# Keys and values brought to token-major form through DRAM squares and VectorE, in a gated delta-rule attention block with a mixture of experts

## The chip, the cores and the metric

The kernel runs on one core of one Trainium2 chip. The metric is the device time of the whole program in microseconds, as the median of several executions. One further execution is recorded by the hardware profiler, and all profile lines come from that one.

## The reference

The program is one layer: layer norm of `x` (2 batches, 2048 tokens, 512 features), plus a gated delta-rule attention, plus a mixture of experts on the first 512 tokens of batch 0.

```python
xn  = layernorm(x)
q = silu(causal_conv4(xn @ Wq) + qcb)      # 16 heads of 128; k and v likewise
k = k * 128 ** -0.5
alpha = sigmoid(xn @ Wa + ba); beta = sigmoid(xn @ Wb + bb)
def step(S, t):                            # per batch and head, over 2048 tokens
    err = S @ k[t] - v[t]
    S = alpha[t] * S - beta[t] * outer(err, k[t])
    o[t] = S @ q[t]
attn = (layernorm_head(o) * ln_w + ln_b) * sigmoid(xn @ Wg) @ Wo
moe  = sum over 4 chosen of 16 experts: down(silu(gate(xn)) * up(xn)) * weight
out  = x + attn + moe
```

Everything is float32.

## The kernel before

The recurrence is done in chunks of 128 tokens (`C`). Inside a chunk the delta rule is a triangular system; its inverse is built from 32 by 32 squares, and only the 128 by 128 state `S` goes from one chunk to the next. A pair is two heads (`HG`), so a batch has 8 pairs; a block is 512 tokens (`BLK`), so a pair has 4 blocks of 4 chunks, and the two batches together have 256 chunks. `recurrence(b, first)` walks over the chunks of a batch, pair by pair, and in every iteration does a little of many things. The order of TensorE, VectorE, ScalarE and GpSimd is written out by hand: each stage is a generator, and `step(...)` in eight slots per iteration advances it. DMAs issued from SP are placed by a scheduler. The stages are:

- `before(n, c)`: what needs no state. In its five first steps it multiplies `q` and `k` (L720), finishes the inverse of the diagonal part (L715, L731, L740, L741, L753), and turns keys and values from feature-major to token-major: four TensorE transposes into one PSUM bank (L735, L736), one ScalarE copy to SBUF (L744), and a GpSimd multiplication that makes `kg` (L750).
- `after(n, c)`, one iteration later: `r` from state and keys (L782, L786), the solve (L793, L797), the new state (L802, L809) and the output `po` (L816, L819), then its mean and variance (L826 to L830). `po` lives in a pool of a single PSUM bank.
- `output(n, c)`, one iteration later still: it normalises `po` (L843), transposes it (L848), gates it (L851, L854) and writes it to DRAM (`oT_d`, L856). It begins with three empty steps, so L843 comes in slot 4.
- `item(n+1, what, h)`: the projection of the next block for q, v or the gate (L156), in halves of two weight tiles; then a causal convolution (`conv_taps`, L131 to L142, and `conv_sum`, three VectorE instructions at L147), then a silu. For q, `gin` (one buffer) is loaded from DRAM by `conv_taps`' caller (L362) and GpSimd multiplies by it (`qg`, L370).
- `key_item(u+2, blk, h)`: the same for keys, two pairs ahead. The keys go to DRAM (`k_d`, L397) and their scores (L206, L210) go to DRAM too (`aT_d`); `inverses` works on those with GpSimd (L246, L249), three steps per iteration in the first ten or so of a pair's sixteen chunks.
- `experts`: the expert matrices (L1154, L1169), four steps per iteration until they are done; `route`: who goes to which expert, in the prologue; `out_chunk`: the last projection by `Wo` (L987), for batch 0 between the two recurrences and for batch 1 woven into the last pair.

`PLAN[c]` names the two items (A, B) of chunk c of a block. A is worked on in slots 2, 4, 5, 6 and 8; B begins in slot 6, becomes `hold`, and is convolved in the next iteration, where `hold` comes in slots 1, 2 and 4. What is left of a generator is drained at the end of the iteration.

`conv_taps` writes the last three tokens of the block before into the front of `raw` with GpSimd (`raw<-halo`, L133), and L147 reads it.

Of the kernel before, what the change touches and what calls it, by code (L numbers as in the profile page):

```python
# [44 lines left out]
def block_kernel(ctx, tc, x, wq, wk, wv, wg, wo, wa, wb, ba, bb, par, consts,  # L45
# [9 lines left out]
    def bank(pool, tag):  # L55
        return pool.tile([P, 512], F32, tag=tag, name=tag)
# [27 lines left out]
    for i in range(1, NQ, 2):  # L84
# [32 lines left out]
           for u in range(NB * NP)]  # L117
    aT_d = [dp.tile([P, NHC, C], F32, name=f"aT_d{u}") for u in range(NB * NP)]
# [169 lines left out]
    PLAN = (("q", 0), ("k", 0)), (("q", 1), ("v", 0)), (("g", 0), ("k", 1)), (("v", 1), ("g", 1))  # L288

    def loads(n):  # L290

        u, blk = blocks[n]
        b = u // NP
        if u not in ws:
            ws[u] = [load_w(bp, tag, w, u % NP * HG, f"{tag}{u}") for tag, w in WS]
        decs = bp.tile([P, HG, CB, DW], F32, tag="decB", name="decB")
        nc.sync.dma_start(
            out=decs, in_=dec_d[b][u % NP][blk].rearrange("p (h c j) -> p h c j", h=HG, c=CB))
        kt = bp.tile([P, HG, BLK], F32, tag="k", name="k")
        nc.sync.dma_start(out=kt, in_=k_d[u][blk].rearrange("h p t -> p h t"))  # L300
        qt = bp.tile([P, HG, BLK], F32, tag="q", name="q")
        qg = bp.tile([P, HG, BLK], F32, tag="qg", name="qg")
        have[n] = (decs, kt, qt, qg, [None] * HG, [])
# [34 lines left out]
    def item(n, what, h, later=None):  # L338


        u, blk = blocks[n]
        b = u // NP
        h0 = (u % NP) * HG
        _, _, qt, qg, vs, _ = have[n]
        ps = bank(ps_p, "p")
        i = "qvg".index(what)
        xt, w = get_xT(b, blk), ws[u][i]
        proj_part(ps, w, h, xt, range(2))
        yield
        proj_part(ps, w, h, xt, range(2, NKT))  # L350
        if (blk, h) == (NBK - 1, HG - 1) and (u + 1) // NP == b:
            tag, w = WS[i]
            ws.setdefault(u + 1, [None] * 3)[i] = load_w(bp, tag, w, (u + 1) % NP * HG, f"{tag}{u + 1}")
        yield
        if what == "g":
            nc.scalar.activation(gate_tile(n)[:, h, :], ps, AF.Tanh, scale=0.5)
            return
        p = 0 if what == "q" else 2
        raw, cv = conv_taps(ps, p, h0, h, blk, later)
        if p == 0:  # L360
            gin = bp.tile([P, BLK], F32, tag="gin", name="gin", bufs=1)
            nc.sync.dma_start(  # L362
                out=gin, in_=gin_d[b][h0 + h, blk * BLK:(blk + 1) * BLK].partition_broadcast(P))
        yield
        conv_sum(raw, cv, p, h0 + h)
        yield
        if p == 0:
            nc.scalar.activation(qt[:, h, :], cv, AF.Silu)  # L368
            yield
            nc.gpsimd.tensor_tensor(qg[:, h, :], qt[:, h, :], gin, ALU.mult)  # L370
        else:
            vs[h] = bp.tile([P, BLK], F32, tag="v", name="v", bufs=4)
            nc.scalar.activation(vs[h], cv, AF.Silu)
# [28 lines left out]
    def projection(n):  # L402

        loads(n)
        for what, h in (("q", 0), ("v", 0), ("q", 1), ("v", 1), ("g", 0), ("g", 1)):
            for _ in item(n, what, h):
                pass
            yield
        load_ops(n)
# [17 lines left out]
    with ExitStack() as es:  # L427
# [34 lines left out]
        def scaled(b, c):  # L462
            mean, r = xns[b, c]
            xn = xns[b, c] = np_.tile([P, HID], F32, tag="xn", name="xn", bufs=3)
            nc.vector.tensor_scalar(xn, xins.pop((b, c)), mean, r, ALU.subtract, ALU.mult)
            if b == 0 and c < FC:
                nc.sync.dma_start(out=xn_d[c * C:(c + 1) * C, :], in_=xn)
# [124 lines left out]
        with tc.manual_schedule(engines={E.PE, E.DVE, E.Activation, E.Pool}):  # L592
            moments(0, 0)
            for g in range(NBK):
                if g + 1 < NBK:
                    moments(0, g + 1)
                if g + 2 < NBK:
                    fetch(0, g + 2)
                for c in range(g * CB, (g + 1) * CB):
                    scaled(0, c)  # L600
                    turned(0, c)
                    if c > 0:
                        gated(0, c - 1)
                if g > 1:
                    key_step(g - 2)
                if 0 < g < 3:
                    key_step(g - 1), key_step(g - 1)
# [16 lines left out]
            r = route(nc, bank, ps_l, mp, cst, cstf[:, N_CONST * P:], topk_idx, topk_w, tw, pos, wrow, trow)  # L624
            inv, firsts = iter(()), []
            for t in range(3, len(keyed) + 3):
                first = t < 11
                old = t - 3
                if t == 11:
                    loads(0)  # L630
                    firsts = [item(0, what, h, later)
                              for what, h in (("q", 0), ("v", 0), ("q", 1), ("v", 1), ("g", 0), ("g", 1))]
# [28 lines left out]
                if first:  # L661
                    n1 += 2
                    if n1 % CB == 0 and n1 // CB + 1 < NBK:
                        fetch(1, n1 // CB + 1)
                        moments(1, n1 // CB + 1)
                    if n1 < NC:
                        scaled(1, n1), scaled(1, n1 + 1)
                if t >= 10:
                    next(r, None)
# [28 lines left out]
    def before(n, c):  # L698
# [4 lines left out]
        decs, kt, qt, _, vs, _ = have[n]  # L703
# [25 lines left out]

        pz = bank(ps_l, "l")  # L730
        nc.tensor.matmul(pz[:, 0:Q], lhsT=op["ihi"][:, c, :], rhs=xs, start=True, stop=True)  # L731

        pkv = bank(ps_l, "l")
        for h in range(HG):
            nc.tensor.transpose(pkv[:, h * D:(h + 1) * D], kt[:, h, cs], ident)  # L735
            nc.tensor.transpose(pkv[:, HW + h * D:HW + (h + 1) * D], vs[h][:, cs], ident)  # L736
# [6 lines left out]
        kv = k2.tile([P, 2, HG, D], F32, tag="kv", name="kv")  # L743
        nc.scalar.copy(kv.rearrange("p s h j -> p (s h j)"), pkv)  # L744
# [4 lines left out]
        kg = k2.tile([P, HG, D], F32, tag="kg", name="kg", bufs=3)  # L749
        nc.gpsimd.tensor_tensor(kg, kv[:, 0], bcast(gd1[b][:, ci, hs], D), ALU.mult)  # L750
# [14 lines left out]
        found[n, c] = (pT, kv, kg, inv)  # L765

    def after(n, c):
# [4 lines left out]
        _, kt, _, qg, _, _ = have[n]  # L772
        pT, kv, kg, inv = found.pop((n, c))
# [3 lines left out]
        if S is None:  # L777
            r = kv[:, 1]
        else:
            pq = bank(ps_c, "c")  # L780
            for h in range(HG):
                nc.tensor.matmul(pq[:, h * D:(h + 1) * D], lhsT=kt[:, h, cs], rhs=S[:, h, :],  # L782
                                 start=True, stop=True)
            r = k2.tile([P, HG, D], F32, tag="r", name="r")
            for h in range(HG):
                nc.vector.scalar_tensor_tensor(  # L786
                    r[:, h, :], pq[:, h * D:(h + 1) * D], gd0[b][:, ci, h0 + h:h0 + h + 1],
                    kv[:, 1, h, :], ALU.mult, ALU.add)
# [44 lines left out]
    def output(n, c):  # L833
# [5 lines left out]
        for _ in range(3):  # L839
            yield  # L840
# [17 lines left out]
    def recurrence(b, first):  # L858
# [13 lines left out]
        mine = {}  # L872
        with tc.manual_schedule(engines={E.PE, E.DVE, E.Activation, E.Pool}):
            for m, at in enumerate([*steps, None, None]):
# [3 lines left out]
                if at:  # L878
# [3 lines left out]
                    if c == 0:  # L882
# [3 lines left out]
                        if blk == 0:  # L886
# [3 lines left out]
                            step(inv)  # L890
                    a = before(n, c)
# [7 lines left out]
                    if u == NB * NP - 1:  # L899

                        if ci == 1:
                            wos = load_wo(b)
                        if ci >= 4:
                            if c == 0:
                                slots.append(big())
                            for _ in last:
                                pass
                            last = out_chunk(b, ci - 4, wos, slots[ci % len(slots)])
                            step(last)
                A, B = pair  # L910
                ps = None

                step(z), step(a), step(hold), step(last)

                step(A), step(z), step(a), step(hold)
# [5 lines left out]
                step(A), step(z), step(a), step(y), step(y), step(y), step(y), step(hold), step(ex)  # L921
# [32 lines left out]
        if slots:  # L954
            for ci in range(NC - 4, NC):
                for _ in out_chunk(b, ci, wos, slots[ci % len(slots)]):
                    pass
# [15 lines left out]
    def out_chunk(b, c, wos, oT):  # L973

        nc.sync.dma_start(out=oT, in_=oT_d[b][c])
        xin = ap.tile([P, HID], F32, tag="aTf", name="xf", bufs=2)
        nc.sync.dma_start(out=xin, in_=x[b, c * C:(c + 1) * C, :])
        if b == 0 and c < FC:
            for j in range(c * TOPK, (c + 1) * TOPK):
                yk = bp.tile([P, HID], F32, tag="v", name="yk", bufs=4)  # L980
# [3 lines left out]
        yield  # L984
        py = bank(ps_p, "p")
        for h in range(H):
            nc.tensor.matmul(py, lhsT=oT[:, h, :], rhs=wos[h], start=(h == 0), stop=(h == H - 1))  # L987
# [8 lines left out]
    slots = [big() for _ in range(NBK - 1)]  # L996
    wos, first = load_wo(0), projection(NP * NBK)
    for c in range(NC):
        for _ in out_chunk(0, c, wos, slots[c % 3 if c < 12 else 1 + c % 2]):
            pass  # L1000
# [6 lines left out]
def route(nc, bank, ps, mp, cst, number, topk_idx, topk_w, tw, pos, wrow, trow):  # L1007
# [29 lines left out]
    run = small("run", NE * n)  # L1037
# [3 lines left out]
    pr = bank(ps, "l")  # L1041
    nc.tensor.matmul(pr[:, 0:NE * n], lhsT=cst[:, K_LT, :], rhs=sel, start=True, stop=False)
    nc.tensor.matmul(pr[:, 0:NE * n], lhsT=cst[:, K_ONE, :], rhs=run, start=False, stop=True)
    pc = bank(ps, "l")
# [19 lines left out]
    at = goes  # L1064
# [37 lines left out]
    pt = bank(ps, "l")  # L1102
# [133 lines left out]
```

## Time and profile before

| | |
|---|---|
| median of 3 executions | 3862.36 us (3862.25 to 3865.29) |
| the profiled execution | 3863.44 us, of it a span of 3861.7 us |
| VectorE, ScalarE, GpSimd busy | 61%, 44%, 44% of the span |
| DMA packets | 583353, of them 354752 under 512 B; 541.36 MB |
| prologue (layer norm, routing, first keys) | 0 to about 245 us |
| recurrence of batch 0, experts until 1377 us | about 245 to 1955 us |
| `Wo` of batch 0 | about 1955 to 2200 us |
| recurrence of batch 1 | about 2200 to 3500 us |
| last pair with `Wo` of batch 1 woven in | about 3500 to 3862 us |

The page gives busy times per engine, the span in 40 slices, the chain of work that ended last, and groups of instructions by line. A float32 matmul is two records in it, and the duration of a record overlaps with that of the next one: the time that a matmul takes from TensorE is the distance between two starts in the timeline, not the duration. In the timeline, `x4` merges four records, and the bracket at the end of a line names the idle time before it and what ended it.

### The profile page before, as it was taken

How to read it: one execution, taken by the hardware profiler on the slowest of the kernel's cores; microseconds unless marked ns; L12 is line 12 of the kernel's file. 1: busy time of each engine (PE TensorE's matmuls, PEld its weight loads, DVE VectorE, ACT ScalarE, POOL GpSimd, SP SyncE). 2: the span in 40 equal slices, each digit the busy share in tenths (PEclk: the TensorE clock that was granted, in tenths of full speed). 3: DMA queues.
4: the chain of work that ended last, by engine and by line, in shares of the span. 5: the costliest groups of instructions: out<-in, count | busy, mean ns of one | idle time of the engine just before them, and what ended most of it. 6: DMA issues, size and time to landing. Idle time of an engine off the chain costs nothing.

```text
span 3861.7 us, 58910 instructions
## 1 busy us (share of the span) xinstructions
PE 3743.5 (97%) x17988; PEld 2439.1 (63%) x17988; DVE 2361.5 (61%) x6136; ACT 1700.4 (44%) x4027; POOL 1690.6 (44%) x3046
## 2 busy tenths in 40 slices
PE   6889999999999999999999999999999999998899
PEld 5557767677676666666654466666666666665454
DVE  5766566665665667777740277777777777663221
ACT  3434444444444455555510155555555555542110
POOL 1246465464654636364520063636363545541010
PEclk9889999999999999999999999999999999999999
DMA  5655656556566554545563335344545444342322
GB/s 162 184 149 162 189 152 190 167 154 191 157 184 170 149 170 108 147 139 163 171 214 113 120 106 139 105 136 112 138 116 127 122 121 133 97 112 76 98 78 88
DMA packets 583353, 541.36 MB, mean 140 GB/s; under 512 B 354752, under 2 KB 425920, under 8 KB 578432
## 3 DMA queue, kind: packets, MB, share of 16 engines
q1 hardware_dynamic: 560928, 456.18, 41.7%
q0 software_dynamic: 22112, 81.41, 7.2%
q8 instruction: 147, 2.41, 0.3%
q14 instruction: 166, 1.36, 0.1%
HBM read 363.69 MB, written 173.67 MB: 139 GB/s over the span
## 4 chain that ended last, share of the span: by engine, by line
PE 84%; DVE 5%; DMA 2%; issue 1%; POOL 1%; ACT 1%; SPq 1%; POOLq 0%; ACTq 0%; DVEq 0%
PE p L156 39%; PE p L987 11%; PE p L1154 4%; DVE cv L147 3%; PE o L816 3%; PE l L720 3%; PE o L819 3%; PE c L793 3%; PE c L802 3%; PE p L206 3%; PE c L782 2%; PE p L1169 2%; PE l L735 1%; PE l L753 1%; PE l L762 1%
## 5 line engine op out<-in xcount | busy, mean ns | idle before, releaser
L147 DVE SCALAR_TENSOR_TENSOR cv<-raw,prm,cv 128x512 f32<-128x512 f32 x1152 | 909.7, 790 | 86.4 <-ACT cv L142 29.5
L156 PE MATMUL p<-xT,wg 128*128 128x512 f32 x1024 | 482.6, 594 | 3.6 <-DVE aTf L210 3.6
L987 PE MATMUL p<-wo,oTf 128*128 128x512 f32 x1024 | 457.9, 602 | 26.4 <-DMA oTf<-oT_d 24.7
L156 PE MATMUL p<-xT,wq 128*128 128x512 f32 x1024 | 482.6, 594 | 0.0
L830 POOL TENSOR_TENSOR rs<-rs,mhalf 128x2 f32<-128x2 f32 x256 | 269.3, 1052 | 483.9 <-DVE rs L829 468.9
L748 POOL COPY inv<-iT 32x32 f32<-32x32 f32 x512 | 103.9, 203 | 861.5 <-DVE iT L740 649.7
L156 PE MATMUL p<-xT,wv 128*128 128x512 f32 x1024 | 481.0, 593 | 0.0
L134 ACT COPY raw<-p 128x512 f32<-128x512 f32 x384 | 223.7, 583 | 525.1 <-PE p L156 510.6
L156 PE MATMUL p<-xT,wk 128*128 128x512 f32 x896 | 431.9, 608 | 16.1 <-DVE aTf L210 11.5
L797 ACT COPY w<-c 128x256 f32<-128x256 f32 x256 | 95.4, 373 | 633.9 <-PE c L793 633.9
L809 DVE SCALAR_TENSOR_TENSOR S<-S,gtot,c 128x128 f32<-128x128 f32 x480 | 145.0, 343 | 357.9 <-PE c L802 357.7
L987 PEld LDWEIGHTS p<-wo,oTf 128*128 128x128 f32 x1024 | 193.1, 193 | 251.1 <-issue 222.7
L249 POOL TENSOR_TENSOR Y<-Y,t 128x30 f32<-128x30 f32 (+14 forms) x480 | 311.0, 648 | 37.6
L142 ACT ACTIVATE cv<-p,prm 128x512 f32<-128x512 f32 x384 | 300.7, 783 | 1.7
L246 POOL TENSOR_TENSOR t<-Y 128x30 f32<-128x30 f32 (+14 forms) x480 | 287.8, 600 | 20.3 <-DMA Y<-aT_d 10.9
L156 PEld LDWEIGHTS p<-xT,wg 128*128 128x128 f32 x1024 | 176.8, 191 | 136.5 <-issue 132.2
L156 PEld LDWEIGHTS p<-xT,wq 128*128 128x128 f32 x1024 | 177.1, 191 | 134.6 <-issue 134.1
L156 PEld LDWEIGHTS p<-xT,wv 128*128 128x128 f32 x1024 | 176.3, 191 | 132.0 <-issue 132.0
L156 PEld LDWEIGHTS p<-xT,wk 128*128 128x128 f32 x896 | 159.6, 196 | 143.5 <-issue 126.3
L786 DVE SCALAR_TENSOR_TENSOR r<-c,gd,kv 128x128 f32<-128x128 f32 x480 | 145.1, 343 | 169.0 <-PE c L782 167.8
L370 POOL TENSOR_TENSOR qg<-q,gin 128x512 f32<-128x512 f32 x128 | 194.3, 1518 | 99.4 <-ACT q L368 99.3
L802 PEld LDWEIGHTS c<-w,kg 128*128 128x128 f32 x1024 | 154.1, 191 | 121.4 <-issue 100.9
(182 smaller groups left out, 7120.8 us busy)
## 6 DMA issues: line engine op xcount, KB each, us to landing
row<-a_d SPq DMA_DIRECT2D x128, 258.0 KB
dec_d<-decA SPq DMA_DIRECT2D x128, 258.0 KB
decB<-dec_d SPq DMA_DIRECT2D x64, 516.0 KB
k_d<-kf SPq DMA_DIRECT2D x128, 256.0 KB
gin<-gin_d SPq DMA_DIRECT2D x128, 256.0 KB
k<-k_d SPq DMA_DIRECT2D x64, 512.0 KB
aT_d<-aTf SPq DMA_DIRECT2D x128, 256.0 KB
oT_d<-oT SPq DMA_DIRECT2D x256, 128.0 KB
```

The costliest lines, as they stand in the source:

```text
L134: nc.scalar.copy(raw[:, KS - 1:], ps)
L142: nc.scalar.activation(cv, ps, AF.Identity, bias=cbias(p, h0 + h), scale=tap(p, h0 + h, KS - 1))
L147: nc.vector.scalar_tensor_tensor(cv, raw[:, j:j + BLK], tap(p, h, j), cv, ALU.mult, ALU.add)
L156: nc.tensor.matmul(ps, lhsT=w[:, k, h * D:(h + 1) * D], rhs=xt[k], start=(k == 0), stop=(k == NKT - 1))
L246: nc.gpsimd.tensor_tensor(t, bass.AP(col.tensor, col.offset, [col.ap[0], (Q, j), (0, n)]), bass.AP(row.tensor, row.offset, [row.ap[0], (0, ...
L249: nc.gpsimd.tensor_tensor(Y[:, 0:j, j + 1:], Y[:, 0:j, j + 1:], t, ALU.add)
L370: nc.gpsimd.tensor_tensor(qg[:, h, :], qt[:, h, :], gin, ALU.mult)
L786: nc.vector.scalar_tensor_tensor(r[:, h, :], pq[:, h * D:(h + 1) * D], gd0[b][:, ci, h0 + h:h0 + h + 1], kv[:, 1, h, :], ALU.mult, ALU.add)
L802: nc.tensor.matmul(pss[:, h * D:(h + 1) * D], lhsT=kg[:, h, :], rhs=w[:, h, :], start=True, stop=True)
L830: nc.gpsimd.tensor_tensor(rs, rs, mhalf[:, 0:HG], ALU.pow)
L987: nc.tensor.matmul(py, lhsT=oT[:, h, :], rhs=wos[h], start=(h == 0), stop=(h == H - 1))
L1154: nc.tensor.matmul(ps[:fn, s, :], lhsT=w[f][:, s, k, :], rhs=xt[:, k, :], start=(k == 0), stop=(k == NKT - 1))
```

## The change

Token-major keys and values are no longer made by TensorE. Each value block is written to DRAM by its item (`v_d`, four blocks in turn), keys are there already, and `squares(n, c)` reads both back for chunk c with eight DMAs of 32 partitions by 8 pieces by 32 numbers (128 bytes a piece). A piece is a row of a 32 by 32 square; the squares land where they belong in the transposed matrix, each still unturned, and one VectorE transpose (which turns 32 by 32 squares in place) for values and one for keys finishes. The four TensorE transposes, the PSUM bank and the ScalarE copy go. `squares` is called two iterations ahead and has three buffers.

For that, values have to come first: `PLAN` and the two other lists of items put v ahead of q, and q0 and q1 now stand as B of chunk 1 and A of chunk 2. `output` loses its three empty steps, and `step(y)` moves to slot 2. In the prologue, the moments and `route` are spread over earlier steps, `route` takes PSUM banks of the tag `p` and the scaling of batch 1 goes from VectorE to GpSimd. The woven `Wo` of batch 1 loads its operand an iteration ahead (`get_out`), in two slots.

```diff
+    v_d = [dp.tile([HG, P, BLK], F32, name=f"v_d{i}") for i in range(4)]
...
-    PLAN = (("q", 0), ("k", 0)), (("q", 1), ("v", 0)), (("g", 0), ("k", 1)), (("v", 1), ("g", 1))
+    PLAN = (("v", 0), ("k", 0)), (("v", 1), ("q", 0)), (("q", 1), ("k", 1)), (("g", 0), ("g", 1))
+    VB = 2
...
+    def squares(n, c):
+
+        u, blk = blocks[n]
+        sq[n, c] = bp.tile([P, 2, HG, D], F32, tag="sq", name="sq", bufs=3)
+        for i, d in enumerate((v_d[n % 4], k_d[u][blk])):
+            for g in range(NQ):
+                o = c * C + g * Q
+                nc.sync.dma_start(
+                    out=sq[n, c][g * Q:(g + 1) * Q, i].rearrange("r h (i j) -> r (h i) j", j=Q),
+                    in_=d[:, :, o:o + Q].rearrange("h (i r) j -> r (h i) j", r=Q))
...
-            vs[h] = bp.tile([P, BLK], F32, tag="v", name="v", bufs=4)
-            nc.scalar.activation(vs[h], cv, AF.Silu)
+            v = bp.tile([P, BLK], F32, tag="v", name="v", bufs=VB)
+            nc.scalar.activation(v, cv, AF.Silu)
+            nc.sync.dma_start(out=v_d[n % 4][h], in_=v)
...
-            nc.vector.tensor_scalar(xn, xins.pop((b, c)), mean, r, ALU.subtract, ALU.mult)
+            (nc.gpsimd if b > 0 else nc.vector).tensor_scalar(
+                xn, xins.pop((b, c)), mean, r, ALU.subtract, ALU.mult)
...
-            r = route(nc, bank, ps_l, mp, cst, cstf[:, N_CONST * P:], topk_idx, topk_w, tw, pos, wrow, trow)
+            r = route(nc, bank, ps_p, mp, cst, cstf[:, N_CONST * P:], topk_idx, topk_w, tw, pos, wrow, trow)
...
-                if t >= 10:
-                    next(r, None)
+                for _ in range({4: 1, 5: 1, 6: 2, 7: 1, 8: 1, 9: 1, 10: 2}.get(t, 0)):
+                    next(r)
...
+        v = k2.tile([P, HG, D], F32, tag="vT", name="vT")
+        kg = k2.tile([P, HG, D], F32, tag="kg", name="kg", bufs=3)
+        for i, t in enumerate((v, kg)):
+            nc.vector.transpose(t.rearrange("p h j -> p (h j)"), sq[n, c][:, i].rearrange("p h j -> p (h j)"))
+
         pz = bank(ps_l, "l")
         nc.tensor.matmul(pz[:, 0:Q], lhsT=op["ihi"][:, c, :], rhs=xs, start=True, stop=True)
-
-        pkv = bank(ps_l, "l")
-        for h in range(HG):
-            nc.tensor.transpose(pkv[:, h * D:(h + 1) * D], kt[:, h, cs], ident)
-            nc.tensor.transpose(pkv[:, HW + h * D:HW + (h + 1) * D], vs[h][:, cs], ident)
         yield
...
-        kv = k2.tile([P, 2, HG, D], F32, tag="kv", name="kv")
-        nc.scalar.copy(kv.rearrange("p s h j -> p (s h j)"), pkv)
...
-        kg = k2.tile([P, HG, D], F32, tag="kg", name="kg", bufs=3)
-        nc.gpsimd.tensor_tensor(kg, kv[:, 0], bcast(gd1[b][:, ci, hs], D), ALU.mult)
+        nc.gpsimd.tensor_tensor(kg, kg, bcast(gd1[b][:, ci, hs], D), ALU.mult)
...
-        for _ in range(3):
-            yield
         o = k2.tile([P, HG, D], F32, tag="o", name="o")
...
+        squares(*steps[0]), squares(*steps[1])
...
+                    if m + 2 < len(steps):
+                        squares(*steps[m + 2])
                     a = before(n, c)
...
+                    if ci > 3:
+                        last = out_chunk(b, ci - 4, wos, *got)
+                    if ci >= 3:
+                        got = get_out(b, ci - 3, slots[(ci - 3) % 2])
...
-                step(A), step(z), step(a), step(hold)
+                step(A), step(z), step(a), step(y), step(hold)
...
-                step(A), step(z), step(a), step(y), step(y), step(y), step(y), step(hold), step(ex)
+                step(A), step(z), step(a), step(hold), step(ex)
...
+    def get_out(b, c, parts):
+
+        heads = []
+        for t, n in parts:
+            o = len(heads)
+            nc.sync.dma_start(out=t, in_=oT_d[b][c][:, o:o + n, :])
+            heads += [t[:, h, :] for h in range(n)]
         xin = ap.tile([P, HID], F32, tag="aTf", name="xf", bufs=2)
         nc.sync.dma_start(out=xin, in_=x[b, c * C:(c + 1) * C, :])
+        return heads, xin
```

## The prediction, made before the changed kernel ran

> **What bounds the kernel.** I read the page's busy times first, then the timeline by engine for two blocks, then the waits, then the chain of waits at the end.
>
> ```profile
> PE 3743.5 (97%) x17988; PEld 2439.1 (63%) x17988; DVE 2361.5 (61%) x6136; ACT 1700.4 (44%) x4027; POOL 1690.6 (44%) x3046
> ...
> PEclk9889999999999999999999999999999999999999
> ```
>
> TensorE is busy all the time at full granted clock, so what leaves its queue counts in full as long as nothing else arrives late. How much leaves must not be read from durations (272 to 289 ns each); starts tell it:
>
> ```profile
> 2459.72 0.31 PE L731 MATMUL l<-xs,ihi 128*128 128x32 f32 x2
> 2459.86 0.31 PE L735 MATMUL l<-unit,k 128*128 128x128 f32 x1
> 2460.00 0.27 PE L736 MATMUL l<-unit,v 128*128 128x128 f32 x1
> 2460.11 0.27 PE L735 MATMUL l<-unit,k 128*128 128x128 f32 x1
> 2460.23 0.27 PE L736 MATMUL l<-unit,v 128*128 128x128 f32 x1
> 2460.33 1.88 PE L156 MATMUL p<-xT,wg 128*128 128x512 f32 x4
> ```
>
> The four transposes take 2460.33 - 2459.86 = 0.47 us. Starts of L782 lie 11.05 and 11.94 us apart in turn without experts (with scores the longer), 14.6 us with them.
>
> **What goes.** Transposes: 256 chunks x 0.47 = **-120**. Two more waits of TensorE go:
>
> ```profile
> PE p L987 <- DMA oTf<-oT_d: 24.7, 6, 8.2
> ...
> PE o L816 <- DVE o L843: 13.8, 21, 1.8
> ```
>
> L843 two slots earlier frees the only `po` bank earlier: **-14**. `Wo`'s operand an iteration ahead: -24.7, and the slow matmuls after these gaps, of which this is the first:
>
> ```profile
> 3509.51 6.54 DMA oTf<-oT_d
> 3516.10 6.58 PE p L987 x8
> ...
> 3525.46 3.44 PE p L987 x8
> ```
>
> 6.58 against 3.44, then 5.67, 5.40, 5.40 and 3.70: -9.6 more, together **-34**. Prologue: VectorE is over 90% busy from 150 to 230 us; routing (about 30 us of it) moves to 90 to 150 us, where VectorE idles some 24 us, and 8 us of scaling go to GpSimd. GpSimd's `inverses` (160 to 223 us) then bound the stretch, so I take **-10** (bounds +5 and -25). Sum -178.
>
> **What comes, and what hides it.** *VectorE*: two 128x256 transposes a chunk. Nearest rows: the 128x32 transpose, 211 ns; copies from PSUM of 32, 128 and 256 columns at 179, 292 and 424 ns, so 1.1 ns a column: 211 + 224 x 1.1 = 0.46; from SBUF less. Bounds 0.3 and 0.9 (two passes); I take 0.42, 0.85 a chunk. They stand just ahead of L740, which waits 208 us in all, 0.81 a chunk, for L731. Counted from L782 in the new order: `r`, `xs` and `pT` end at 1.7, the two L843 at 2.4, `hold`'s convolution (2.45) at 4.85, transposes at 5.7, `top` at 5.95; L753 needs it at 6.48. Covered, with half a microsecond to spare. Without that cover a chunk would pay what the transposes run over. The new `PLAN` puts two convolutions in both chunk 1 and chunk 2 (before: 1 and 3), so chunk 2 needs 11.1 us of VectorE (5.1 and two times 2.42 for convolutions and 1.15 for `decA`) in TensorE's 10.6; chunk 3 starts half a microsecond late on VectorE. That lies inside the wait found below and is not counted twice. ScalarE's 150 us of copies (L744) and the PSUM bank go at no gain: neither is waited for. `kg` comes from SBUF and no later.
>
> *DMA engines*: per chunk 8 x 256 pieces of 128 bytes. Nearest row: the loads of `Y` (same pieces) at 252 to 256 us, where queue 1 had
>
> ```profile
> q1 hardware_dynamic: 3360, 0.42, 69.6%
> ```
>
> 0.696 x 4 us x 16 engines / 3360 = 13.3 ns a packet; 2048 x 13.3 / 16 = 1.7 us a chunk, and 0.4 for writing v. The windows show a share of 0.45 in batch 1 (5.2 us a chunk) and 0.59 beside experts: 7.3 of 11, not a bound. The Trainium skill ("VectorE: DVE Perf Modes", The three transpose paths) speaks against it: a plain DMA that transposes by its access pattern is 19 times slower than the crossbar. By that rule, 256 KB at its 435 GB/s (my estimate, from "DMA: Bandwidth & Descriptors", Specifications) x 19 = 11 us a chunk, on top of 5.2: 16 us, over 1100 us slower. I take the row: 32 numbers stay contiguous on both sides here.
>
> *SP*: its issues in batch 1 sum to 22.5 us per block of 46.2; 34 more at 0.5 (`Y`'s: 0.48, plus 0.04) make 39.5 of 44: tight. SP also stands until a `v_d` write has landed before it loads those squares, some 2.5 us a time, with `oT_d`, `inv` and `row` behind it; but nothing in its queue is wanted sooner than an iteration later, except `gin`. At the first handover (240 to 262 us), where SP issues without a pause, 16 of the 24 first squares stand ahead of `X_d` and cost nothing; the rest is within the prologue's bounds.
>
> *GpSimd and gin*: here I expect the new wait. `gin` has one buffer. Before, q0 and q1 ended in different iterations; now both are drained at the end of chunk 2, and the built order has `qg x2` adjacent on GpSimd, q1's `gin` load waiting on GpSimd on SP, and behind both `qg` the `raw<-halo` copy that chunk 3's convolution (k1) on VectorE waits for, with both transposes, L740, L741 and so L753 behind it. One `qg` already costs VectorE a wait, in this chunk with experts (started 787.31):
>
> ```profile
> 788.09 1.28 POOL L370 TENSOR_TENSOR qg<-q,gin 128x512 f32<-128x512 f32 x1
> 789.30 0.19 POOL L133 COPY raw<-halo 128x3 f32<-128x3 f32 x1
> ```
>
> and on VectorE
>
> ```profile
> 789.53 2.81 DVE L147 SCALAR_TENSOR_TENSOR cv<-raw,prm,cv 128x512 f32<-128x512 f32 x3 [0.47 <-POOL raw L133]
> ```
>
> A `gin` load: issued 2318.89, its traffic is the last block of
>
> ```profile
> DMA  0079931999994000044445564335520000210721
> ```
>
> (2318 to 2323 us, 0.125 a slice), ending at 2321.75: 2.9, with receipts 3.1. Without experts, the first `qg` ends 1.95 after chunk 3's L782 where inverses stand ahead of it (from the one at 2456.40), load at 5.15, second `qg` 6.4, `raw` 6.6, convolution 9.1, transposes 9.95, `top` 10.2; L753's turn is at 6.48: TensorE stands 3.75. In a pair's last block, without inverses (1.85 less), 1.9. Mean 0.75 x 3.75 + 0.25 x 1.9 = 3.3. Beside experts: the row above plus 4.4 gives `raw` 793.7, `top` 797.5 against L753's 796.84 - 0.47: 1.15 in three of four, about 1 with GpSimd's expert requests. Blocks with keys to make: 56, of which 20 beside experts (until 1377 us). **+118 and +20.** Bounds: 0 (if the load is quick or VectorE late anyway) and 5 us a block (280).
>
> Clock: the skill ("TensorE: Matmul & The Clock Gate", Why this matters for your kernels) wants no gaps over about 3 us. Rows: gaps of 5.4 to 6.5 cost 0.3 to 3.1, one of 1.14 cost 0.2 (10.57 for 24 matmuls, 10.3 otherwise). By the rule 27 gaps of 3.75 would pay some 1.9 each, 51; I take 0.2, **+5**, since 3.75 is nearer the cheap side of these rows.
>
> **Sum.** -178 + 138 + 5 = -35. The profiled execution had 3863.4 (span 3861.7), 1 us over the median: 3863 - 35 = **3828**.
>
> **Rivals.**
> - *The wait is absorbed* (bound 0): 3863 - 178 = 3685. For it: VectorE has 13% left. Against: the order on three engines is fixed, and the round trip has no other cover. 0.16.
> - *SP becomes the bound*, the slower side. Place: blocks of batch 1 and the 12 of batch 0 after the experts. At 0.76 an issue (four `ihi` loads behind a megabyte of `X_d` writes took 3.05) a block takes 22.5 + 34 x 0.76 = 48.3 instead of 46.2: 40 x 2.1 = +84, with tail, prologue and expert blocks -60: 3885; at 1 us an issue 56.5 a block, 4200. It decides above (46.2 - 22.5) / 34 = 0.70 an issue. For it: each DMA reuses one of eight semaphores and waits for the eighth before it. Against: `Y`'s eight in a row went at 0.54. 0.20.
> - *Transposes at 0.9*: +0.95 a chunk; chunks 1 and 2 lose 0.5 each (+40), chunk 3 one (+50): 3918. 0.12.
> - That the transposes stay on TensorE is excluded by the built order, which has 1024 fewer.
>
> **Numbers.** Forecast 0.52 (3790 to 3865 is its own range). The range 3700 to 3940 leaves out most of the first rival and SP's far end. Within 0.2% (8 us) is what this measurement can't tell from no change. Faster: 0.44 of the forecast's, 0.16, 0.02 = 0.62; same 0.04 + 0.02 + 0.02 = 0.08; slower 0.04 + 0.16 + 0.10 = 0.30.
>
> **What will show it.** L735 and L736 gone and L731 followed by L156 0.14 later; a TensorE wait at L753 (or its weights) for VectorE's `top` in one chunk of four, about 3 us, and GpSimd idle before the second `qg` by a DMA of `gin`, about 60 times 3; no `oTf` wait; L816's wait gone; the 128x256 transposes near 0.4; SP's issues of `sq` near 0.5. Wrong would be: GpSimd not idle before `qg`, or TensorE waiting for `ilo`, `inv`, `row` or `sq`, which would be SP or the DMA engines.

## The result, and the profile after

The changed kernel takes **4188.5 us** (median of 4 runs, 4183.5 to 4199.3) against 3862.3 us before on the same chip: ratio **1.085**, 95% interval 1.083 to 1.088. It is slower by 326 us; 3828 was forecast, with a range that ended at 3940.

First the page of the kernel after (engine, busy time, share, instructions; then the granted TensorE clock in 40 slices):

```profile
PE 3749.3 (90%) x16964; PEld 2393.1 (57%) x16964; DVE 2559.2 (61%) x6632; ACT 1541.0 (37%) x3771; POOL 1672.6 (40%) x3062
...
PEclk9989999999999999999999999999999999999999
```

The instructions fell as announced (17988 to 16964 on TensorE), yet TensorE is as long busy as before (3749 us against 3744; the slow clock below ate the saving) and idle for another 432 - 118 = 314 us: the span grew from 3861.7 to 4181.7. The mean granted clock fell from 0.989 to 0.953. A view of the waits (engine, tile, line, releaser: us in total, times, longest) says where it stands:

```profile
PE l L769 <- DVE top L760: 306.5, 56, 13.9
PE c L502 <- POOL xn L481: 22.8, 5, 11.0
```

L769 is the old L753. It stands for `top` 56 times: in the last chunk of 55 of the 56 blocks with keys to make, and once more, for 1.68 us, in another chunk. The chain behind it is in the same view of GpSimd and of VectorE:

```profile
POOL qg L385 <- DMA gin<-gin_d: 376.6, 62, 13.2
...
DVE cv L148 <- POOL raw L134: 248.3, 45, 13.3
```

So the second `qg` (old L370) waits for its `gin`, VectorE's convolution waits for the `raw<-halo` copy behind that `qg` (in a pair's first block for the zeros in its place, L132: 67.9 us in 15), and TensorE waits for what VectorE does after it. That is the wait foretold, but 5.5 us a time (306.5 / 56) and not 3.3 without experts and 1.0 beside them. One such chunk, in the timeline of TensorE (start, us, line, records merged, and in brackets the idle time before):

```profile
2541.89 0.39 PE L835 MATMUL o<-S,qg 128*128 128x128 f32 x2
2552.42 0.77 PE L769 MATMUL l<-top,a 128*128 128x128 f32 x2 [10.14 <-DVE top L760]
2552.98 0.63 PE L862 MATMUL c<-unit,o 128*128 128x128 f32 x2
2553.40 3.36 PE L157 MATMUL p<-xT,wg 128*128 128x512 f32 x4
```

After 10.14 us of standing the next four projection matmuls take 3.36 us; four in a chunk without a wait take 1.88. For stretches around another wait, of 3.39 us and ending at 2494.8, the view by windows gives (columns: length; busy us of PE, PEld, DVE, ACT and POOL; granted clock; DMA share; GB/s):

```profile
2480.00:2495.00 15.00, 10.68 (x48) 6.37 (x47) 12.45 (x26) 5.65 (x16) 9.42 (x14) 1.00 0.51 121
2494.80:2498.40 3.60, 3.52 (x8) 2.02 (x9) 2.27 (x9) 2.42 (x7) 3.28 (x7) 0.53 0.36 98
2500.00:2512.00 12.00, 12.00 (x55) 7.46 (x54) 7.28 (x22) 5.23 (x14) 4.59 (x10) 1.00 0.56 132
```

For 3.6 us after the wait about half of the clock is granted (0.53), then all of it again: this wait is paid for twice.

Why 10 us and not 3? On SP, before that wait (start, duration of the issue, what it loads):

```profile
2538.29 0.42 SPq L181 DMA_DIRECT2D row<-a_d  x1
2538.85 0.37 SPq L299 DMA_DIRECT2D decB<-dec_d  x1
2539.31 0.38 SPq L258 DMA_DIRECT2D X_d<-X  x1
2539.74 1.01 SPq L329 DMA_DIRECT2D a<-aT_d  x1
2540.85 0.85 SPq L329 DMA_DIRECT2D ihi<-X_d  x1
2541.79 0.72 SPq L377 DMA_DIRECT2D gin<-gin_d  x1
```

The first `qg` had ended at 2538.95, itself a microsecond late (last section). Three issues of the handover from pair to pair stand between, so `gin` goes out 2.84 us late, and behind that traffic it takes 5.81 until the second `qg` starts at 2547.60. In the other blocks of batch 1 with keys to make it goes out within half a microsecond, with one exception (1.0), and the start follows 3.4 to 5.1 us later.

By stages, from the starts of L720 (after: L739), one per chunk (us; before, then after):

| stage | before | after | difference |
|---|---|---|---|
| prologue | 240.8 | 239.2 | -1.6 |
| first 80 chunks, with experts | 1176.4 | 1285.7 | +109.3 |
| other chunks of batch 0 | 533.6 | 626.4 | +92.8 |
| `Wo` of batch 0 | 254.4 | 254.2 | -0.2 |
| batch 1 to the last pair | 1252.8 | 1406.8 | +154.0 |
| last 16 chunks | 320.6 | 290.6 | -30.0 |
| rest | 83.1 | 78.8 | -4.3 |

The sum is +320, the difference of the spans. Only the recurrences lost.

### The profile page after: what moved, and what is told of

The parts are those of the page before. It is cut to its first block, busy times and chain, and to the rows that moved or that the text cites. A ratio compares the mean times of both kernels' runs of the same rounds, so it can differ in the third digit from the quotient of the medians.

```text
span 4181.7 us, 60444 instructions
## 1 busy us (share of the span) xinstructions
PE 3749.3 (90%) x16964; PEld 2393.1 (57%) x16964; DVE 2559.2 (61%) x6632; ACT 1541.0 (37%) x3771; POOL 1672.6 (40%) x3062
## 3 DMA queue, kind: packets, MB, share of 16 engines
q1 hardware_dynamic: 1138720, 556.98, 49.9%
## 4 chain that ended last, share of the span: by engine, by line
PE 68%; DMA 12%; DVE 6%; SPq 4%; issue 3%; POOL 3%; ACT 1%; DVEq 0%; POOLq 0%; ACTq 0%
PE p L157 33%; PE p L1022 10%; PE p L1188 3%; PE p L207 2%; PE l L739 2%; DMA gin<-gin_d 2%; PE c L809 2%; PE c L798 2%; PE c L818 2%; PE l L769 2%; PE o L832 2%; PE p L1203 2%; DVE cv L148 2%; PE o L835 2%; PE c L862 1%
## 5 line engine op out<-in xcount | busy, mean ns | idle before, releaser
L157 PE MATMUL p<-xT,wg 128*128 128x512 f32 x1024 | 550.4, 666 | 3.5 <-DVE aTf L211 3.5
L157 PE MATMUL p<-xT,wv 128*128 128x512 f32 x1024 | 490.7, 602 | 0.0
L157 PE MATMUL p<-xT,wq 128*128 128x512 f32 x1024 | 486.1, 598 | 1.1 <-ACT cv L143 1.1
L157 PE MATMUL p<-xT,wk 128*128 128x512 f32 x896 | 426.7, 602 | 2.6 <-DVE aTf L211 2.6
L769 PE MATMUL l<-top,a 128*128 128x128 f32 x512 | 116.0, 311 | 307.7 <-DVE top L760 306.5
L764 ACT COPY bot<-iT 32x32 f32<-32x32 f32 x512 | 110.2, 215 | 740.3 <-DVE iT L759 732.4
L846 POOL TENSOR_TENSOR rs<-rs,mhalf 128x2 f32<-128x2 f32 x256 | 259.1, 1012 | 267.9 <-DVE rs L845 259.0
L1022 PE MATMUL p<-wo,oTf 128*128 128x512 f32 x768 | 335.9, 593 | 1.2 <-DMA wo<-in_wo 1.2
L385 POOL TENSOR_TENSOR qg<-q,gin 128x512 f32<-128x512 f32 x128 | 178.3, 1393 | 382.8 <-DMA gin<-gin_d 376.6
L157 PEld LDWEIGHTS p<-xT,wg 128*128 128x128 f32 x1024 | 198.9, 214 | 159.4 <-issue 155.2
L247 POOL TENSOR_TENSOR t<-Y 128x30 f32<-128x30 f32 (+14 forms) x480 | 263.4, 549 | 19.0 <-DMA Y<-aT_d 6.5
L769 PEld LDWEIGHTS l<-top,a 128*128 128x128 f32 x512 | 84.7, 208 | 320.3 <-issue 316.5
L157 PEld LDWEIGHTS p<-xT,wv 128*128 128x128 f32 x1024 | 178.4, 193 | 135.6 <-issue 135.3
L157 PEld LDWEIGHTS p<-xT,wq 128*128 128x128 f32 x1024 | 176.8, 191 | 134.3 <-issue 131.1
L1022 PEld LDWEIGHTS p<-wo,oTf 128*128 128x128 f32 x768 | 143.6, 190 | 170.9 <-issue 168.6
```

The source lines that it names most:

```text
L157: nc.tensor.matmul(ps, lhsT=w[:, k, h * D:(h + 1) * D], rhs=xt[k], start=(k == 0), stop=(k == NKT - 1))
L247: nc.gpsimd.tensor_tensor(t, bass.AP(col.tensor, col.offset, [col.ap[0], (Q, j), (0, n)]), bass.AP(row.tensor, row.offset, [row.ap[0], (0, ...
L769: nc.tensor.matmul(px[:, 0:C], lhsT=op["a64"][:, c, :], rhs=wide(top[:, 0:64]), start=True, stop=True)
L846: nc.gpsimd.tensor_tensor(rs, rs, mhalf[:, 0:HG], ALU.pow)
L1022: nc.tensor.matmul(py, lhsT=heads[h], rhs=wos[h], start=(h == 0), stop=(h == H - 1))
```

## The experiments

**Two ways out of the round trip, and the round trip alone.** The question of the first four runs was whether the loss is the pairing of the two `qg` or the squares.

e1: two buffers for `gin`, room taken from `v`.

```diff
-    VB = 2
+    VB = 1
-            gin = bp.tile([P, BLK], F32, tag="gin", name="gin", bufs=1)
+            gin = bp.tile([P, BLK], F32, tag="gin", name="gin", bufs=2)
-                yk = bp.tile([P, HID], F32, tag="v", name="yk", bufs=VB)
+                yk = bp.tile([P, HID], F32, tag="gin", name="yk", bufs=2)
```

> The changed kernel with two buffers for gin instead of one (the room comes from v, one buffer instead of two; the output stage's gathered rows share gin's two). Theory G (the second qg's load waits for the first qg, and TensorE's standing at L769 also lowers its clock): the waits of TensorE for top (306.5 us in 56) and the slower clock (about 150 us) go together: 3690 to 3770 us, granted clock back to 0.98 or more, GpSimd's wait for gin under 60 us. Rival S (SP is behind, and the round trip only shows it): the issue of gin stays 3 to 6 us late in one block of four, TensorE waits for something else in its place: over 3880 us. Rival C (the lower clock has nothing to do with the gaps): only the waits go, about 3880 us, granted clock still near 0.95.

Measured: **4002 us** (ratio to before 1.037, 1.036 to 1.039), clock 0.970, no wait for `gin` left among the longer ones; TensorE's waits for `top` are 60.7 us in 58. It is better by 186 us, but far from the 3770 of theory G. The run is not clean, as ScalarE's waits show:

```profile
ACT v L388 <- DMA v_d<-v: 186.0, 33, 12.1
```

With one `v`, ScalarE stood until the write of v to DRAM had landed, up to 12 us. What I took from `v` for `gin` made a wait of its own.

e2: the same aim without a byte more, by the list alone. q0 and q1 end in different iterations.

```diff
-    PLAN = (("v", 0), ("k", 0)), (("v", 1), ("q", 0)), (("q", 1), ("k", 1)), (("g", 0), ("g", 1))
+    PLAN = (("v", 0), ("v", 1)), (("q", 0), ("k", 0)), (("q", 1), ("k", 1)), (("g", 0), ("g", 1))
```

> The changed kernel with one buffer for gin as it was, but the list of projections reordered so that q0 and q1 end in different iterations: (v0, v1), (q0, k0), (q1, k1), (g0, g1). The convolutions per iteration stay 1, 2, 2, 1. Theory G: no round trip is left, so as good as two buffers: 3690 to 3770 us, no wait of GpSimd for gin over 60 us in sum. Rival V (VectorE is too full in the iterations with two convolutions, and the wait for top comes from there): the waits for top stay, over 4000 us. Rival S as above: over 3880 us.

Measured: **3954 us** (1.025, 1.023 to 1.026), clock 0.973. So one line of the list is worth 4188.5 - 3954.0 = 235 us. But it is far from the 3690 to 3770 of theory G: something else costs. Of GpSimd's and TensorE's waits:

```profile
POOL qg L385 <- DMA gin<-gin_d: 129.5, 29, 11.7
```

```profile
PE l L769 <- DVE top L760: 92.2, 45, 10.4
```

e3: the opposite. The kernel before, with nothing but the changed list.

```diff
-    PLAN = (("q", 0), ("k", 0)), (("q", 1), ("v", 0)), (("g", 0), ("k", 1)), (("v", 1), ("g", 1))
+    PLAN = (("v", 0), ("k", 0)), (("v", 1), ("q", 0)), (("q", 1), ("k", 1)), (("g", 0), ("g", 1))
```

> The kernel before with nothing but the changed list of projections (values first, q0 and q1 both drained in iteration 2); transposes stay on TensorE, no squares, SP as little loaded as before. Theory G: about 56 waits of TensorE at the first product with top, 3 to 4 us each without SP's lateness (180 to 220 us), and 60 to 100 us of slower clock: 4080 to 4180 us. Rival Q (the loss comes from the squares: their issues on SP, their traffic, or the transposes on VectorE): within 10 us of 3862.

Measured: **4278 us** (1.109, 1.107 to 1.110), clock 0.953. The list alone costs 418 us, more than the whole change and more than theory G's 4180, and rival Q is refuted as the cause of the main loss. TensorE stands at the output instead, because `o` (L843) is behind the same convolution here:

```profile
PE o L816 <- DVE o L843: 297.7, 57, 12.4
```

```profile
POOL qg L370 <- DMA gin<-gin_d: 294.1, 54, 8.7
```

One thing I had expected wrongly: I put the 10-us blocks down to squares on SP. They are here too, without any squares (in one block of four in batch 1, `gin` goes out 2.5 to 2.7 us late and the second `qg` starts 5.8 to 6.0 us after that). They come from the handover.

e4: e2 with keys and values turned by TensorE and held in SBUF as before. What stays of the change is prologue, tail, the earlier output steps and the list of e2.

```diff
-        for i, t in enumerate((v, kg)):
-            nc.vector.transpose(t.rearrange("p h j -> p (h j)"), sq[n, c][:, i].rearrange("p h j -> p (h j)"))
+        pkv = bank(ps_l, "l")
+        for h in range(HG):
+            nc.tensor.transpose(pkv[:, h * D:(h + 1) * D], kt[:, h, cs], ident)
+            nc.tensor.transpose(pkv[:, HW + h * D:HW + (h + 1) * D], vs[h][:, cs], ident)
...
-                        squares(*steps[m + 2])
```

> The reordered list of the run before, but keys and values turned by TensorE and held in SBUF as in the kernel before; prologue, tail and the earlier output steps stay changed. Against the reordered list with squares it shows what the squares alone are worth. Theory G with the prediction's sum (256 times 0.47 = 120 us of TensorE saved, nothing lost): 110 to 130 us slower than the reordered list with squares, 3800 to 3870 us. Rival Q: not slower than the one with squares.

Measured: **3828 us** (0.992, 0.990 to 0.993), clock 0.993, and no wait of TensorE over 22 us in sum. It is within G's range in itself, but the comparison falls the other way, as rival Q had it: without squares it is 126 us *faster* than with them. Even with the round trip parted, the squares cost more than the four transposes that they save. That was new, and the next runs are about it.

**What the squares cost.** Distances in us between the starts of L739 in successive chunks, in two consecutive blocks of batch 1, worked out from the timelines (e9 and e13 come below):

```
e4  without squares        10.60 10.60 11.94 11.94 | 11.04 11.05 12.84 12.53
e2  with squares           10.21 10.21 20.10 11.55 | 10.66 10.66 13.07 13.21
e9  squares, no loads      10.21 10.22 11.56 12.70 | 10.66 10.66 13.07 13.21
e13 nor VectorE transposes 10.22 10.21 11.55 11.55 | 10.66 10.66 12.48 12.55
```

The 20.10 of e2 is a chunk in which `gin` was late again (TensorE stood 5.45 us for `top`). A chunk with nothing in its way is shorter by 0.39 us (10.60 to 10.21, 11.05 to 10.66): that is what TensorE's four transposes really took, 256 x 0.39 = 100 us. From 3828 - 100 = 3728 to e2's 3954 there are 226 us to explain.

e9: e2, loading only the first three chunks' squares.

```diff
+        if len(sq) > 2:
+            sq[n, c] = list(sq.values())[len(sq) % 3]
+            return
```

> The reordered list with squares, but only the first three chunks' squares of the whole kernel are loaded; all later chunks transpose these again, so their keys and values are left out of the state (the writes of v to DRAM stay). VectorE's transposes, the missing transposes of TensorE and all else stay. Theories S1 and S2 (the loads cost it): 3720 to 3750 us. Theory S3 (VectorE): 3900 us or more.

Measured: **3795 us** (0.983, 0.981 to 0.984). The loads cost 159 of the 226; 67 stay. The rows above show where: 12.70 for 11.94, 13.07 and 13.21 for 12.84 and 12.53.

e13: e9 without VectorE's transposes.

```diff
-        for i, t in enumerate((v, kg)):
+        for i, t in enumerate(fresh):
...
-        nc.gpsimd.tensor_tensor(kg, kg, bcast(gd1[b][:, ci, hs], D), ALU.mult)
+        nc.gpsimd.tensor_tensor(kg, once[1], bcast(gd1[b][:, ci, hs], D), ALU.mult)
```

(`once` holds two transposed tiles, made in the first chunk; `fresh` is those two there and empty later.)

> The run without loads after the first three chunks (3795 us), with VectorE's two transposes left out too after the first chunk, so that keys and values of all chunks but the first are left out of the state. What is left is TensorE without its four transposes and VectorE as in the kernel before. If the 67 us between 3795 and 3728 (3828 less 256 times 0.39) are VectorE's transposes, which have no room in iterations with two convolutions: 3720 to 3740 us, and the chunks of 12.2, 12.7, 13.1, 13.2 and 13.7 us fall to 11.6 to 12.5. If not (order, writes of v, missing copies on ScalarE): 3780 us or more.

Measured: **3749 us** (0.970, 0.969 to 0.972). Of the 67 us, 46 are VectorE's transposes; without them the long chunks fall to 11.55 to 12.55. Some 20 us above 3728 remain unexplained, and the expectation (3740 at most) was missed by 9 us.

For what the loads cost there were two theories, S1 (SP's queue) and S2 (traffic); S3 (VectorE) is priced above.

e5: the four key loads of a chunk from ScalarE's queue.

```diff
-                nc.sync.dma_start(
+                (nc.scalar if i else nc.sync).dma_start(
                     out=sq[n, c][g * Q:(g + 1) * Q, i].rearrange("r h (i j) -> r (h i) j", j=Q),
```

> The reordered list with squares (3954 us), with the four loads of the key squares of each chunk issued from ScalarE's queue instead of SP's: same bytes, same pieces, 1024 issues fewer on SP. Theory S1 (what the squares still cost, 226 us against the 3728 that 3828 less 256 times 0.39 gives, is SP's queue: gin and the handover's loads are issued late): at least half of it goes, 3850 us or less. Theory S2 (it is the traffic of 128-byte pieces on the DMA engines): 3930 to 3970 us. Theory S3 (it is VectorE, whose transposes have no room in the iterations with two convolutions): 3930 to 3970 us. If ScalarE's own work is held up by the issues (some 1.8 us a chunk), TensorE waits for w or inv instead, and the time is over 3970.

Measured: **4103 us** (1.062, 1.060 to 1.063). ScalarE's own work stood behind the issues:

```profile
ACT raw L135 <- DMA sq<-k_d: 300.8, 86, 9.6
```

Relieving SP this way moves the queue onto an engine that computes, and says nothing of S1.

e7: `gin` early, ahead of the squares, with two buffers (and again one `v`). e8: e7 with e5's edit. e10: `gin` early with one buffer and two of `v`.

```diff
+                    if c in (0, 2) and n + 1 < n0 + NP * NBK:
+                        load_gin(n + 1, c // 2)
                     if m + 2 < len(steps):
                         squares(*steps[m + 2])
```

(that is e10; e7 and e8 have `c < HG` and `c`; `load_gin` makes the tile and issues the load that `item` made before.)

> The reordered list with squares, two buffers for gin and its load issued one iteration before its projection, ahead of that iteration's squares; all else as it was, all squares on SP. Theory S1: gin no longer stands behind squares on SP, so GpSimd's waits for gin (129.5 us in 29) go, and with them the long waits for top: 3800 to 3880 us. Theory S2 and S3: the waits for gin go, but TensorE's time stays over 3920 us, since something else is late in its place.

> Both of these together: gin early, key squares issued by ScalarE. Theory S1: the best of the three, 3730 to 3800 us, and below the version without squares (3828). Theories S2 and S3: over 3920 us.

> The reordered list with squares (3954 us), one buffer for gin and two for v as there; only the two loads of gin are issued earlier, ahead of the squares of iterations 0 and 2. The run with gin early and two buffers also cut v to one buffer, and ScalarE then waited 171.6 us for the writes of v; here that is undone. Theory S1 (gin behind squares and handover loads on SP is what the loads cost): GpSimd's wait for gin under 40 us instead of 129.5, time 3820 to 3890 us. Rival S2 (traffic slows whatever is loaded, so the lateness moves to another load): no better than 3930 us.

Measured: e7 **3984** (1.033), e8 **4076** (1.056), e10 **3963** (1.026, 1.024 to 1.027), none better than e2's 3954. In e7 ScalarE's wait for the write of v is back (171.6 us in 48), as in e1; so e7 was confounded, and e10 is the clean run. There the lateness moved: in e2 and in e10 VectorE waited for `row`

```profile
DVE decA L198 <- DMA row<-a_d: 18.8, 10, 5.4
```

```profile
DVE decA L198 <- DMA row<-a_d: 103.0, 28, 10.6
```

(first e2, then e10), and `gin` was still waited for, 171.0 us in 34. That `gin` had one buffer is not the reason: SP stood no longer at its issue than in e2 (58.7 us in all, against 61.4). Putting one load ahead in a queue that is behind puts another one late. So it isn't the place of `gin` on SP, which was S1 in its narrow form.

e12: all issues, an eighth of the bytes (one of eight pieces per partition; `k` is 1 after the first three chunks).

```diff
-                    out=sq[n, c][g * Q:(g + 1) * Q, i].rearrange("r h (i j) -> r (h i) j", j=Q),
-                    in_=d[:, :, o:o + Q].rearrange("h (i r) j -> r (h i) j", r=Q))
+                    out=sq[n, c][g * Q:(g + 1) * Q, i].rearrange("r h (i j) -> r (h i) j", j=Q)[:, 0:k],
+                    in_=d[:, :, o:o + Q].rearrange("h (i r) j -> r (h i) j", r=Q)[:, 0:k])
```

> The reordered list with squares, where after the first three chunks each of the eight loads per chunk brings only one of its eight pieces per partition (4 KB instead of 32), so most of every chunk's keys and values are stale and left out of the state; the number of issues on SP and their waits for the writes of v stay. No loads at all gave 3795, all loads 3954. Theory S1 (issues and waits on SP): 3900 to 3960 us. Theory S2 (traffic of 128-byte pieces): 3790 to 3820 us.

Measured: **3882 us** (1.005, 1.003 to 1.007), between the two expectations. 3882 - 3795 = 87 us come with the issues and their waits, 3954 - 3882 = 72 with the bytes. The split is rough, since the waits were not quite kept (SP stands 218 us at these loads, 259 in e2). Neither theory alone is right.

e11: keys alone by squares, values by TensorE; nothing fresh is waited for, and half the issues and half of VectorE's work go. It is e4 with four loads a chunk, issued one iteration ahead, in two buffers.

```diff
+        kg = k2.tile([P, HG, D], F32, tag="kg", name="kg", bufs=3)
+        nc.vector.transpose(kg.rearrange("p h j -> p (h j)"), sq[n, c][:, 0].rearrange("p h j -> p (h j)"))
...
-            nc.tensor.transpose(pkv[:, h * D:(h + 1) * D], kt[:, h, cs], ident)
-            nc.tensor.transpose(pkv[:, HW + h * D:HW + (h + 1) * D], vs[h][:, cs], ident)
+            nc.tensor.transpose(pkv[:, h * D:(h + 1) * D], vs[h][:, cs], ident)
```

> The version without squares (3828 us) with the keys alone taken from squares: four loads a chunk, one transpose on VectorE, two of the four transposes on TensorE and no write of v to DRAM. Half of the gain in TensorE is 50 us (256 times 0.195). Theory S1: SP has room for half the issues and nothing waits for a fresh write, VectorE has room for one transpose: 3775 to 3810 us, faster than both. If the losses are of any load of squares: 3828 us or more.

Measured: **3805 us** (0.986, 0.984 to 0.987), clock 0.990: faster than the kernel before by 56 us, than the changed one by 384, and than e4 by 24, about half of the 50 us that two transposes fewer save on TensorE. From its page:

```profile
PE 3686.0 (97%) x17476; PEld 2382.3 (63%) x17476; DVE 2464.7 (65%) x6376; ACT 1630.7 (43%) x4027; POOL 1713.7 (45%) x3062
```

TensorE is busy 97% again, with 512 instructions fewer than before.

## Why the prediction was wrong, step by step

The forecast named the wait that decided, and sized it wrongly: its sum was -35, and +326 was measured. The first two terms below are the ones that failed; the others are small, or held.

- **The wait for `gin` was mis-sized**: +138 foretold, 306.5 measured. The place (second `qg`, `raw`, convolution, transposes, `top`, L753), the number of blocks (56, of which 55 show it), and the part after `qg` were right: TensorE resumes 4.8 to 5.3 us after the second `qg` starts, 5.05 foretold. Wrong was what lies before it. I took one undisturbed load (3.1 us) as the round trip; the trace of after has 3.4 us at best, often 5 to 6, and SP up to 6.6 us late with the issue. In the 18 blocks of batch 1 outside the handover the waits are 3.2 to 4.2 us, 3.5 on the mean, near the 3.3 foretold (in part by luck: in a pair's last blocks 3.6, where 1.9 was foretold). In its six handover blocks they are 10.1: SP is 2.6 to 3.4 us late there, and the load takes 5.2 to 6.0, and the prediction had neither. Over both batches the 37 waits without experts have a mean of 5.7 (3.3 foretold), the 19 beside experts 5.0 (1 foretold). The bound of 5 us a block was too low as well, since it held no late SP. e2 and e3 show the cause by taking the round trip away and by adding it alone.
- **The clock was mis-sized**: +5 foretold, about +90 measured. TensorE is busy for 246 us in the stretches that the trace of after grants at half the clock, for 67 us in those of before; at half speed half of that is lost, so 123 less 33 is an estimate of 90. A second reckoning comes near: in the 24 blocks of batch 1 with this wait the chunk takes 19.40 us; less all its waits (5.57) and less the same chunk of e13 (11.83), 2.0 us remain. Here I weighed the rule against rows (0.3 to 3.1 us for gaps in the tail, 0.2 for one of 1.14 us) and took the cheap end. The Trainium skill ("TensorE: Matmul & The Clock Gate", Why this matters for your kernels) was the better guide: no gaps over about 3 us. At 1.9 us a gap, what I got by the rule, 56 gaps make 106. Not every gap pays. The same page (What's actually happening) says that the window for it is free-running, which fits two waits at the same place in two pairs. One of 3.70 us cost 0.2 (the chunk takes 15.49, less 3.70: 11.79; the clock stays at 1.00 for the 3.6 us after it). One of 3.22 cost 3.1 (17.84, less 3.22: 14.62; the clock is at 0.50 for 3.6 us). Both chunks take 11.55 in e13. No run kept the wait and changed the clock alone; the tie is read from the clock in the windows.
- **What TensorE saves**: 100, not 120. From the timeline of TensorE after:

```profile
2464.21 0.31 PE L755 MATMUL l<-xs,ihi 128*128 128x32 f32 x2
2464.36 1.96 PE L157 MATMUL p<-xT,wv 128*128 128x512 f32 x4
```

  L157 follows L755 (before: L731) at once, as foretold, but its four take 1.96 us here and not the 1.88 that stood behind the transposes. That 0.08 a chunk is what my reading of starts left out.
- **The prologue**: -1.6 for -10. TensorE comes to the first chunk and stands 15.7 us for `ilo`, where it stood 1.3. The squares ahead of `X_d` did cost nothing, as counted: e4, without any, stands 15.1. GpSimd's `inverses` bound the stretch, as foretold, but they end only 2.6 us earlier (their last copy starts at 221.0 instead of 223.6), and TensorE waits for what follows them.
- **VectorE was covered, as foretold**: the half microsecond late was to vanish in the wait found, "not counted twice". In 54 of the 56 chunks with a wait for `top` VectorE had itself stood for `raw`, so it was not behind. The transposes are as foretold too (0.437 and 0.402 us at the median). Only where the wait is parted does their cost come to light, as the 46 us between e9 and e13.
- Right: the tail (-30 and -4 in the last two rows of the table for the -34 foretold, though some 6 of it are the transposes of its 16 chunks), and the `oTf` wait gone; L816's wait for L843 gone (13.8 us before); issues of squares at 0.45 us.

The two traces close by themselves: TensorE stands 314 us longer, 306.5 of them for `top`, loses some 90 more to the slow clock, and the rest of its busy time is 84 shorter, which makes the 320. Of the 100 that the transposes save, 16 are thus not placed.

Of the rivals, *SP becomes the bound* was half right. Its size (3885 to 4200) fits e2, its rule (0.70 an issue) doesn't: issues of squares took 0.45 us at the median and 0.46 on the mean, only 66 of 2048 over 0.70, and no even slowing of all blocks is seen. Lateness comes in bursts, at handovers and beside experts, and only where a load is wanted at once. *Absorbed* at 3685 was out of reach even without the round trip; without loads and VectorE transposes too it is 3749. *Transposes at 0.9* is refuted. The weighing of the transposing DMA went as I took it: no 11 us a chunk. From the pages of before and after, queue 1 took 41.7% of 3861.7 us and 49.9% of 4181.7, so 1.9 us more a chunk for 2.1 foretold, and all the loads cost 159 / 256 = 0.6 us of time. The Trainium skill ("VectorE: DVE Perf Modes", The three transpose paths) gives its 19 times for a large innermost stride at the destination; here that stride is one number, so it did not speak against the squares.

## What to carry to other kernels

Before moving work between lists, mark every single-buffered load, and see whether two of its users have come into one step: a round trip to DRAM that nothing covers was worth 418 us here, and one line of order gave back 235. Price such a wait with the latest issue of its queue and the load beside other traffic, not by an undisturbed load, and add the slow clock after it. What is taken off the bounding engine has to fit into the next ones at their fullest step: half of the transposes moved (keys, which lie ready) gained 24 us, all of them lost 126.

## What else the runs showed

VectorE's scan and GpSimd's work take longer side by side. In the handover block of the kernel after:

```profile
2534.82 1.98 POOL L256 COPY X<-Y 128x1024 f32<-128x1024 f32 x1
2536.74 2.21 POOL L385 TENSOR_TENSOR qg<-q,gin 128x512 f32<-128x512 f32 x1
```

```profile
2534.86 3.03 DVE L198 TENSOR_TENSOR_SCAN decA<-row,decA 128x516 f32<-128x516 f32 x1
```

The scan takes 3.03 us where its median is 1.23, and the `qg` 2.21 where its median is 1.27. The Trainium skill ("SBUF — State Buffer", SBUF: two separate sides) has a VectorE instruction with two SBUF inputs and GpSimd share a port pair that one of them holds for a whole instruction; the scan reads two, and waiting for the copy to end before it starts would give about these 3 us. No run parted the two. The overlap makes the first `qg`, and so the round trip, a microsecond later in just the blocks that wait longest.
